# Six of sixteen denominator sums moved from the vector engine to accumulating DMA transfers, with value buffers and early weight work rearranged

## The chip, the cores and the metric

The kernel runs on one core of a Trainium2 chip. The metric is the device time of the whole program in microseconds (us), and lower is better. The time before the change is 3305.59 us, the median of three runs that lie between 3302.00 and 3307.45 us. Five engines work side by side, each in its own program order: PE (matrix products, with PEld for its weight loads), DVE (vector operations), ACT (activations), POOL (GpSimd) and SP (here only an issuer of DMA transfers). They wait for each other by semaphores.

## What is computed

The input is 4 images of 64x64 positions with 256 channels, in fp32. Two layers follow each other:

```python
# layer 0: attention of every position over all 4096 of its image
q = x @ Wq + bq; k = x @ Wk + bk; v = x @ Wv + bv
energy = jnp.einsum('bnd,bmd->bnm', q, k)
attn = softmax(energy, axis=-1)
out = gamma * jnp.einsum('bnm,bmc->bnc', attn, v) + inputs
# layer 1: 3x3 depthwise convolution (three outputs a channel), two pointwise
# layers with a GELU between, a residual, then 3x3 windowed attention and a residual
```

The part that matters here is the softmax of layer 0. The kernel takes exponentials without subtracting a maximum, multiplies them by the values, and divides at the end by the sum of the exponentials, the denominator. `gamma` and the value bias `b_v` enter only where the finished sum is scaled and added to the input.

## The kernel before

The 4 x 4096 positions are cut into 32 **slots** of 512 queries, 8 slots to an image. One slot walks over the 4096 keys of its image in 16 **points** of 256 keys each; a point is named by `G` (0 to 7, a block of 512 keys) and `half`. Number n below is 2G + half. In the loop over points the code writes, in this order: the loads (`load_keys` two blocks ahead, `load_values`, `spread_queries`), `high_part` and `energy` for later points, `load_forms`, the slot's jobs for the second layer (`jobs[point]`, of slots three to five earlier), the product of this point, the sum of the denominators, steps of the depthwise convolution on DVE (`perceive`), and on some slots projections of the next image.

- `energy` (L371) makes two matrix products into a PSUM tile `e`, of which there is one, and ACT's exponential writes `p` (L383), 128 x 1024 numbers. It is called two points ahead of the product, and there are three `p` buffers. So the exponential of n+3 can only be written when everything that reads p of n has ended.
- `product` (L393) adds the values times `p` into PSUM accumulators. At the seven even points 2, 4, ..., 14 of most slots (`IN_PARTS`; not in slots 0, 2 and 31) it does so in three parts, for which DVE makes `pl` (L430) and `pg` (L435) from `p` and ACT's `ph` (L388).
- `add_up` (L421) adds `p` of each point to `den` on DVE (L433). At point 14 it adds p of n = 15 and folds the two halves of `den` (L440). At point 15 `partial_sums` (L450) transposes and reduces `den` to `parts` (L458, L459), together with `lsum`, a sum that POOL makes at point 12 (L1010 to L1020) from masked weights (L991). `finish` (L473) then multiplies `parts` on PE (L477, `dps`), and PE comes to that product straight after point 15.
- `load_values` (L296) fetches a block's values into `v`. There are three such buffers, and the load for block G+2 is written at the start of block G. `load_forms` (L310) fetches the two other forms of the values into `vf`, two buffers, 512 KB a load, three points ahead.
- In slot 0 the values, keys and queries are still being projected (`project_v` L317, `project_qk` L254). `gamma` and `b_v` are loaded on SP's queue just ahead of the first slot (L1107, L1109), and DVE multiplies them at once (L1110, L1112). `clear_tap` (many tiny DVE operations on the convolution's weights) stands at points 5 to 7 of slot 0, and `turn_weights` (four DVE operations of 0.75 us on `wup`, L679) at points 9 to 14. At point 8 of slot 1 POOL stores and reloads weights and makes `wmix` (`mix_weights`, L637).

Each engine executes its instructions in the order in which this code writes them, so a waiting instruction holds up all that is behind it on its engine. A tile with several buffers takes them in turn, and the first write to a buffer waits for its last reader. The lines around the change:

```python
            if half == 0:
                ahead = slot + (G + 2) // NG, (G + 2) % NG
                if ahead[0] < NSLOT:
                    load_keys(*ahead)
                if 0 < ahead[0] < NSLOT:
                    load_values(*ahead)
```

Of the kernel before, what the change touches and what calls it, by code (L numbers as in the profile page):

```python
# [12 lines left out]
ALU = mybir.AluOpType  # L13
# [3 lines left out]
P = 128  # L17
B, H, W, C = 4, 64, 64, 256
# [4 lines left out]
NB = 512  # L23
# [4 lines left out]
TPB = NB // P  # L28
# [5 lines left out]
MULT = 3  # L34
# [5 lines left out]
NG = NT // GRP  # L40
SQ = 32
NJ = NB // SQ
NSLOT = B * NBLK
# [6 lines left out]
SPLIT = 4096.0  # L50
BELOW = 1.0 - 2.0**-13
IN_PARTS = (2, 4, 6, 8, 10, 12, 14)


LAG_PERC, LAG_HID, LAG_ATT = 2, 3, 5
# [3 lines left out]
def attention_then_perception_kernel(  # L59
# [23 lines left out]
    def loaded(src, name, shape=None, queue=None):  # L83
        t = const.tile(list(shape or src.shape), F32, tag=name, name=name)
        (queue or nc.sync).dma_start(out=t, in_=src)
        return t
# [10 lines left out]
    def unshifted():  # L97
# [6 lines left out]
        def tile_of(shape, tag, name, bufs=1):  # L104
            return pool.tile(shape, F32, tag=tag, name=name, bufs=bufs)
# [188 lines left out]
            load_parts(keys[s, G], block(s, G), 1)  # L294

        def load_values(s, G):  # L296
            values[s, G] = tile_of([P, TPB, C], "v", f"v_{s}_{G}", 3)
            to = values[s, G].rearrange("p t c -> p (t c)")
            at = 2 * block(s, G)
            if not any(in_parts(s, G, half) for half in range(2)):  # L300
                nc.sync.dma_start(out=to, in_=packed_v[:, bass.ds(at * 2 * C, TPB * C)])
                return
            for half in range(2):
                if in_parts(s, G, half):
                    of = packed_f[:, at + half, 0]
                else:
                    of = packed_v[:, bass.ts(at + half, 2 * C)]
                nc.sync.dma_start(out=to[:, bass.ts(half, 2 * C)], in_=of)
# [11 lines left out]
        def project_v(s, pair, tag="m"):  # L320
            xc = staged[s]
            ps = bank(tag, f"v_{s}_{pair}")
            for i in range(2):
                for kin in range(CH):
                    nc.tensor.matmul(  # L325
                        ps[:, i * C : (i + 1) * C],
                        lhsT=xc[:, kin, bass.ts(2 * pair + i, P)], rhs=wv[:, kin, :],
                        start=(kin == 0), stop=(kin == CH - 1),
                    )
            of = ps.rearrange("p (t c) -> p t c", c=C)  # L330
            split = 2 * (s % NBLK) + pair in IN_PARTS
            if not split or s < NBLK or s >= NSLOT - NBLK:
                if s >= NBLK:
                    v = fresh(f"vs_{s}_{pair}")
                else:
                    if (0, s) not in values:
                        values[0, s] = tile_of([P, TPB, C], "v", f"v_0_{s}", 3)
                    v = values[0, s][:, 2 * pair : 2 * pair + 2, :]
                nc.scalar.activation(v, of, AF.Identity, scale=SPLIT / (SPLIT + 1.0))  # L339
                nc.scalar.dma_start(  # L340
                    out=packed_v[:, bass.ts(2 * s + pair, 2 * C)],
                    in_=v.rearrange("p t c -> p (t c)"),
                )
            if split:
                low, high = (fresh(f"v{n}_{s}_{pair}") for n in "lh")
                nc.scalar.copy(low, of)
                nc.scalar.activation(high.bitcast(F32R), of, AF.Identity, scale=BELOW)
                nc.vector.tensor_tensor(low, low, high, ALU.subtract)
                gap = fresh(f"vg_{s}_{pair}")
                nc.vector.scalar_tensor_tensor(gap, low, -SPLIT, high, ALU.mult, ALU.add)  # L350
                nc.vector.tensor_scalar(low, low, SPLIT, None, ALU.mult)
                for i, part in enumerate((high, low, gap)):
                    nc.gpsimd.dma_start(
                        out=packed_f[:, 2 * s + pair, i], in_=part.rearrange("p t c -> p (t c)")
                    )
# [9 lines left out]
            load_parts(queries[s], s, 0)  # L365


        weights, highs, lows, gaps = {}, {}, {}, {}
        sums, accs, lsums, lrdens = {}, {}, {}, {}
        parts_, inverses, turneds = {}, {}, {}  # L370

# [2 lines left out]
        def energy(s, G, half):  # L374

            e = epsum.tile([P, 2, NB], F32, tag="e", name=f"e_{s}_{G}_{half}", bufs=1)
            for i in range(2):
                nc.tensor.matmul(  # L378
                    e[:, i, :], lhsT=keys[s, G][:, bass.ts(2 * half + i, P)].bitcast(F32R),
                    rhs=queries[s].bitcast(F32R), start=True, stop=True,  # L380
                )
            p = tile_of([P, 2, NB], "p", f"p_{s}_{G}_{half}", 3)
            nc.scalar.activation(p, e, AF.Exp)  # L383
            weights[s, G, half] = p
# [6 lines left out]
        def product(s, G, half):  # L391
# [17 lines left out]
            for part, (w, to, x) in enumerate((  # L409
                (v, 0, highs[s, G, half]), (f[:, :2], 0, lows[s, G, half]), (f[:, 2:], CH, gaps[s, G, half])  # L410
            )):
                for i in range(2):
                    for c in range(CH):
# [4 lines left out]
                            stop=(to > 0 and n == len(IN_PARTS) - 1 and i == 1),  # L418
                        )

        def add_up(s, G, half):  # L421

            p = weights[s, G, half]
            if G == 0 and half == 0:
                sums[s] = tile_of([P, 2, NB], "den", f"den_{s}")
                return
            if in_parts(s, G, half):
                high = highs[s, G, half]
                low, gap = (tile_of([P, 2, NB], f"p{n}", f"p{n}_{s}_{G}_{half}") for n in "lg")
                nc.vector.tensor_tensor(low.bitcast(F32R), p, high, ALU.subtract)  # L430
            den = sums[s]
            before = weights[s, 0, 0] if (G, half) == (0, 1) else den
            nc.vector.tensor_tensor(den, before, p, ALU.add)  # L433
            if in_parts(s, G, half):
                nc.vector.scalar_tensor_tensor(  # L435
                    gap.bitcast(F32R), low, -SPLIT, high, ALU.mult, ALU.add
                )
                lows[s, G, half], gaps[s, G, half] = low, gap
            if G == NG - 1 and half == 1:
                nc.vector.tensor_tensor(den[:, 0, :], den[:, 0, :], den[:, 1, :], ALU.add)  # L440

        def squares(t):
# [104 lines left out]
            return thirds.pop(0)  # L547

        def spare(s, name):
            if s == NSLOT - 1:  # L550
                return tile_of([P, TPB, C], "v", name, 3).rearrange("p (a t) c -> p a (t c)", a=2)
            spares.append(spares.pop(0))
            return tile_of([P, 2, NB], spares[-1], name)

        spares = ["ph", "pl", "pg"]

        def perceive(s, steps):

# [115 lines left out]
        def turn_weights(n, half):  # L674
            p, q, _ = ROUNDS[n]
            up, uq = (wup1[:, half * MULT + i, :] for i in (p, q))
            swap, back, m = (coef[:, n, i, half : half + 1] for i in range(3))
            for to, k, of in ((uq, back, up), (up, swap, uq), (uq, back, up), (up, m, uq)):
                nc.vector.scalar_tensor_tensor(to, of, k, to, ALU.mult, ALU.add)  # L679
# [424 lines left out]
            project_v(2, i)  # L1104
        fetch(4)
        fetch(5)
        gam = loaded(gamma.partition_broadcast(P), "gam", [P, 1])  # L1107

        gbv = loaded(b_v.rearrange("o (c p) -> p (o c)", p=P), "gbv")  # L1109
        nc.vector.tensor_scalar(gbv, gbv, gam[:, 0:1], None, ALU.mult)  # L1110
        gam_parts = pool.tile([P, 1], F32, tag="gam_parts", name="gam_parts")
        nc.vector.tensor_scalar(gam_parts, gam, 1.0 + 1.0 / SPLIT, None, ALU.mult)  # L1112
        wlv = pool.tile([P, CH, C], F32, tag="wlv", name="wlv")
        combine = combine_steps()

# [8 lines left out]
        for slot in range(NSLOT):  # L1124
# [51 lines left out]
            for point in range(points):  # L1176
                G, half = divmod(point, 2)
                after = slot + (G + 1) // NG, (G + 1) % NG
                if half == 0:
                    ahead = slot + (G + 2) // NG, (G + 2) % NG  # L1180
                    if ahead[0] < NSLOT:
                        load_keys(*ahead)
                    if 0 < ahead[0] < NSLOT:
                        load_values(*ahead)
                    if G == NG // 2 and slot + 1 < NSLOT:
                        spread_queries(slot + 1)
                behind = slot + (point + 1) // points, *divmod((point + 1) % points, 2)
# [1 line left out]
                    high_part(*behind)  # L1189
                if after[0] < NSLOT:  # L1190
                    energy(*after, half)
                soon = slot + (point + 3) // points, *divmod((point + 3) % points, 2)
                if in_parts(*soon):
                    load_forms(*soon)
# [23 lines left out]
                if slot == 0 and point == 1:  # L1218
# [3 lines left out]
                    wperc, bperc = wb[:, :, :, :TAPS], wb[:, :, :, TAPS]  # L1222
                    wup1 = loaded(w_up1, "wup1", queue=nc.gpsimd)
                    bup1 = loaded(b_up1, "bup1", queue=nc.gpsimd)
                if slot == 0 and NG - MULT <= point < NG:
                    if point == NG - MULT:
                        scratch = tile_of([P, NB], "rden", "scratch")
                        scratch = scratch[:, : (TAPS + 3) * CH].rearrange("p (j c) -> p j c", c=CH)
                        nc.vector.tensor_copy(bperc, bias)
                    clear_tap(point - NG + MULT)  # L1230
                if slot == 0 and NG < point <= NG + 2 * MULT:
                    turn_weights(*divmod(point - NG - 1, 2))
                if slot == 0 and point == NG:

                    next(combine)
# [485 lines left out]
```

## Time and profile before

| | |
|---|---|
| median of three runs | 3305.59 us |
| the profiled execution, its whole time | 3305.77 us |
| its span, first to last instruction | 3304.1 us |
| mean granted clock of PE | 0.997 |
| PE busy | 3264.6 us |
| DVE busy | 2905.2 us |
| ACT busy | 1349.2 us |
| POOL busy | 500.7 us |
| denominator sums L433 `den<-den,p`, 448 of them | 564.9 us of DVE |
| DMA, mean rate | 124 GB/s |

1.7 us of the profiled execution lie outside its span. "Busy" counts an engine's own work; issuing a DMA or waiting is not in it for SP and ACT, while POOL's row contains its own DMA issues. In lines of a timeline the first number is the start in us from the span's start, the second the length of the merged run of instructions, then come engine, source line, operation, the tile written `<-` the tiles read, and the count; in brackets stands how long the engine had been idle, and what ended the wait.

### The profile page before, as it was taken

How to read it: one execution, taken by the hardware profiler on the slowest of the kernel's cores; microseconds unless marked ns; L12 is line 12 of the kernel's file. 1: busy time of each engine (PE TensorE's matmuls, PEld its weight loads, DVE VectorE, ACT ScalarE, POOL GpSimd, SP SyncE). 2: the span in 40 equal slices, each digit the busy share in tenths (PEclk: the TensorE clock that was granted, in tenths of full speed). 3: DMA queues.
4: the chain of work that ended last, by engine and by line, in shares of the span. 5: the costliest groups of instructions: out<-in, count | busy, mean ns of one | idle time of the engine just before them, and what ended most of it. 6: DMA issues, size and time to landing. Idle time of an engine off the chain costs nothing.

```text
span 3304.1 us, 35658 instructions
## 1 busy us (share of the span) xinstructions
PE 3264.6 (99%) x11986; PEld 2170.4 (66%) x11986; DVE 2905.2 (88%) x4243; ACT 1349.2 (41%) x1647; POOL 500.7 (15%) x627
## 2 busy tenths in 40 slices
PE   8999999999999999999999999999999999999998
PEld 5556666666666666676666666666666666666655
DVE  4788899888999999987999999998799999999894
ACT  3334444444444444444444444444444444444331
POOL 2200011120111110112001111101210011111121
PEclk9999999999999999999999999999999999999999
DMA  6533333464333433346333333435643333333100
GB/s 207 184 113 108 115 115 117 143 193 139 117 115 122 128 116 114 117 149 209 117 116 117 115 122 121 128 105 174 200 130 103 121 112 115 122 122 121 48 18 27
DMA packets 246910, 410.90 MB, mean 124 GB/s; under 512 B 92272, under 2 KB 93312, under 8 KB 246592
## 3 DMA queue, kind: packets, MB, share of 16 engines
q1 hardware_dynamic: 231632, 370.15, 36.8%
q0 software_dynamic: 7408, 24.95, 1.9%
q10 hardware_dynamic: 7680, 13.44, 1.1%
q8 instruction: 99, 1.62, 0.2%
q14 instruction: 91, 0.75, 0.1%
HBM read 346.92 MB, written 60.69 MB: 123 GB/s over the span
## 4 chain that ended last, share of the span: by engine, by line
PE 92%; DVE 4%; DMA 1%; ACT 1%; issue 1%; SPq 0%; POOL 0%; ACTq 0%; DVEq 0%; POOLq 0%
PE acc L402 30%; PE acc L414 16%; PE e L378 7%; PE dx L762 6%; PE hid_bc L705 5%; PE hid_gf L705 5%; PE hid_de L705 5%; PE lv L925 3%; PE g L858 3%; PE v L325 3%; PE lo L1059 3%; PE s L966 2%; PE hid_a L705 2%; DVE perc L592 2%; PE qk L259 1%; PE hid L737 1%
## 5 line engine op out<-in xcount | busy, mean ns | idle before, releaser
L402 PE MATMUL acc<-p,v 128*128 128x512 f32 x2472 | 1113.5, 593 | 0.2 <-ACT v L339 0.2
L592 DVE SCALAR_TENSOR_TENSOR perc<-xp,wb,perc 128x526 f32<-128x526 f32 (+1 forms) x1356 | 969.1, 773 | 0.1
L383 ACT ACTIVATE p<-e 128x1024 f32<-128x1024 f32 x512 | 524.3, 1024 | 1054.3 <-PE e L378 888.0
L402 PEld LDWEIGHTS acc<-p,v 128*128 128x128 f32 x2472 | 466.8, 190 | 486.8 <-issue 472.5
L433 DVE TENSOR_TENSOR den<-den,p 128x1024 f32<-128x1024 f32 x448 | 564.9, 1261 | 1.0 <-ACT p L383 0.6
L991 POOL TENSOR_TENSOR lp<-lp,near 128x396 f32<-128x396 f32 x60 | 150.8, 2513 | 1965.3 <-ACT lp L986 1965.3
L378 PE MATMUL e<-qa,ka 128*128 128x512 f32 x1024 | 427.9, 499 | 13.0 <-ACT p L383 13.0
L378 PEld LDWEIGHTS e<-qa,ka 128*128 128x128 f32 x1024 | 190.0, 190 | 162.7 <-issue 128.0
L388 ACT ACTIVATE ph<-p 128x1024 fp32r<-128x1024 f32 x203 | 214.4, 1056 | 199.4 <-PE acc L414 130.5
L414 PE MATMUL acc<-ph,v 128*128 128x512 f32 x812 | 264.4, 447 | 0.0
L430 DVE TENSOR_TENSOR pl<-p,ph 128x1024 fp32r<-128x1024 f32 x203 | 253.2, 1247 | 12.1 <-ACT ph L388 12.0
L435 DVE SCALAR_TENSOR_TENSOR pg<-pl,ph 128x1024 fp32r<-128x1024 f32 x203 | 256.7, 1264 | 0.0
L762 PE MATMUL dx<-hid,wup 128*128 128x512 f32 x512 | 229.8, 592 | 0.0
L414 PE MATMUL acc<-pg,vf 128*128 128x512 f32 x812 | 222.0, 395 | 1.1 <-DVE pg L435 1.1
L414 PE MATMUL acc<-pl,vf 128*128 128x512 f32 x812 | 219.6, 392 | 0.0
L414 PEld LDWEIGHTS acc<-ph,v 128*128 128x128 f32 x812 | 148.3, 189 | 51.0 <-issue 26.8
L414 PEld LDWEIGHTS acc<-pg,vf 128*128 128x128 f32 x812 | 152.5, 188 | 37.0 <-DVE pg L435 1.5
L414 PEld LDWEIGHTS acc<-pl,vf 128*128 128x128 f32 x812 | 152.7, 188 | 35.6 <-DVE pl L430 0.4
L598 DVE TENSOR_TENSOR perc<-perc 128x262 f32<-128x262 f32 x360 | 168.0, 481 | 6.3
L1014 POOL TENSOR_TENSOR lsum<-lsum,lp 128x99 f32<-128x99 f32 (+1 forms) x179 | 171.8, 966 | 11.7
L728 ACT ACTIVATE hid<-hid,bup 128x512 f32<-128x512 f32 x120 | 80.1, 715 | 215.8 <-DVE hid L712 215.8
L762 PEld LDWEIGHTS dx<-hid,wup 128*128 128x128 f32 x512 | 96.8, 190 | 98.6 <-issue 93.4
(203 smaller groups left out, 3872.4 us busy)
## 6 DMA issues: line engine op xcount, KB each, us to landing
vf<-packed_f SPq DMA_DIRECT2D x203, 512.0 KB, 4.1
ka<-packed SPq DMA_DIRECT2D x1016, 64.0 KB, 3.0
v<-packed_f SPq DMA_DIRECT2D x203, 256.0 KB, 2.7
v<-packed_v SPq DMA_DIRECT2D x203, 256.0 KB, 2.9
v<-packed_v SPq DMA_DIRECT2D x45, 512.0 KB, 3.5
xp<-in_x SPq DMA_DIRECT2D x30, 528.0 KB, 6.8
xc<-in_x SPq DMA_DIRECT2D x56, 256.0 KB, 3.8
out<-lo SPq DMA_DIRECT2D x56, 256.0 KB, 2.0
```

The costliest lines, as they stand in the source:

```text
L378: nc.tensor.matmul(e[:, i, :], lhsT=keys[s, G][:, bass.ts(2 * half + i, P)].bitcast(F32R), rhs=queries[s].bitcast(F32R), start=True, stop= ...
L383: nc.scalar.activation(p, e, AF.Exp)
L388: nc.scalar.activation(high.bitcast(F32R), weights[s, G, half], AF.Identity, scale=BELOW)
L402: nc.tensor.matmul(accs[s][c], lhsT=v[:, i, bass.ts(c, P)], rhs=p[:, i, :], start=(first and i == 0), stop=(last and i == 1),)
L414: nc.tensor.matmul(accs[s][to + c], lhsT=w[:, i, bass.ts(c, P)].bitcast(F32R), rhs=x[:, i, :].bitcast(F32R), start=(to > 0 and n == 0 and ...
L430: nc.vector.tensor_tensor(low.bitcast(F32R), p, high, ALU.subtract)
L433: nc.vector.tensor_tensor(den, before, p, ALU.add)
L435: nc.vector.scalar_tensor_tensor(gap.bitcast(F32R), low, -SPLIT, high, ALU.mult, ALU.add)
L592: nc.vector.scalar_tensor_tensor(acc, win, wt, acc, ALU.mult, ALU.add)
L705: nc.tensor.matmul(ps[:, n * C : (n + 1) * C], lhsT=w(j), rhs=rows_of(mixes[s, j][:, kind, :]), start=(j == 0), stop=(j == MULT - 1),)
L762: nc.tensor.matmul(ps, lhsT=wup2[:, d, bass.ts(c, P)], rhs=hids[s][:, d, :], start=(d == 0), stop=(d == NHC - 1),)
L1014: nc.gpsimd.tensor_tensor(to, to, near_ws[block, half][:, t_, of, :], ALU.add)
```

## The change

Six of the sixteen sums of a slot, n = 3, 5, 7, 9, 11 and 13 in slots 1 to 30, leave DVE. POOL issues a transfer of `p` into a new tile `sent` instead: a plain copy for n = 3, and transfers that add to what is there for the others. One DVE addition at the end joins `sent` to `den`. The tile `v` has two buffers instead of three, and a block's values are loaded one block ahead instead of two. In slot 0 the eight tiles of values alternate between `v` and `vf`, two buffers each, and of the tiles that slot 31's convolution borrows the third is now a `vf`. `gamma` and `b_v` are loaded after point 1 of slot 0 and multiplied at point 3; `clear_tap` stands at points 3 to 5 instead of 5 to 7, `turn_weights` at points 6 to 11 instead of 9 to 14.

```diff
+BY_DMA = (3, 5, 7, 9, 11, 13)
...
-            values[s, G] = tile_of([P, TPB, C], "v", f"v_{s}_{G}", 3)
+            values[s, G] = tile_of([P, TPB, C], "v", f"v_{s}_{G}", 2)
...
-                        values[0, s] = tile_of([P, TPB, C], "v", f"v_0_{s}", 3)
+                        values[0, s] = tile_of([P, TPB, C], ("v", "vf")[s % 2], f"v_0_{s}", 2)
...
+        def by_dma(s, n):
+            return 0 < s < NSLOT - 1 and n in BY_DMA
+
+        def send(s, n):
+            p = weights[s, n // 2, n % 2]
+            if n == BY_DMA[0]:
+                sent[s] = tile_of([P, 2, NB], "sent", f"sent_{s}")
+                nc.gpsimd.dma_start(out=sent[s], in_=p)
+            else:
+                nc.gpsimd.dma_start(out=sent[s], in_=p, accum_op=ALU.add)
+
         def add_up(s, G, half):
 
+            if by_dma(s, 2 * G + half):
+                return
...
             if G == NG - 1 and half == 1:
+                if s in sent:
+                    nc.vector.tensor_tensor(den, den, sent.pop(s), ALU.add)
                 nc.vector.tensor_tensor(den[:, 0, :], den[:, 0, :], den[:, 1, :], ALU.add)
...
-        gam = loaded(gamma.partition_broadcast(P), "gam", [P, 1])
-
-        gbv = loaded(b_v.rearrange("o (c p) -> p (o c)", p=P), "gbv")
-        nc.vector.tensor_scalar(gbv, gbv, gam[:, 0:1], None, ALU.mult)
         gam_parts = pool.tile([P, 1], F32, tag="gam_parts", name="gam_parts")
-        nc.vector.tensor_scalar(gam_parts, gam, 1.0 + 1.0 / SPLIT, None, ALU.mult)
...
-                    if 0 < ahead[0] < NSLOT:
-                        load_values(*ahead)
+                    if 0 < after[0] < NSLOT:
+                        load_values(*after)
...
                 if after[0] < NSLOT:
                     energy(*after, half)
+                if by_dma(slot, point + 1):
+                    send(slot, point + 1)
...
                     bup1 = loaded(b_up1, "bup1", queue=nc.gpsimd)
-                if slot == 0 and NG - MULT <= point < NG:
-                    if point == NG - MULT:
+                    gam = loaded(gamma.partition_broadcast(P), "gam", [P, 1])
+                    gbv = loaded(b_v.rearrange("o (c p) -> p (o c)", p=P), "gbv")
+                if slot == 0 and MULT <= point < 2 * MULT:
+                    if point == MULT:
+                        nc.vector.tensor_scalar(gbv, gbv, gam[:, 0:1], None, ALU.mult)
+                        nc.vector.tensor_scalar(gam_parts, gam, 1.0 + 1.0 / SPLIT, None, ALU.mult)
...
-                    clear_tap(point - NG + MULT)
-                if slot == 0 and NG < point <= NG + 2 * MULT:
-                    turn_weights(*divmod(point - NG - 1, 2))
+                    clear_tap(point - MULT)
+                if slot == 0 and 2 * MULT <= point < 4 * MULT:
+                    turn_weights(*divmod(point - 2 * MULT, 2))
```

`after` is the block one ahead, (G+1) of the slot, or block 0 of the next slot.

More of the change, by code (lines that the diff above doesn't have):

```diff
@@ L365, in spread_queries @@
             load_parts(queries[s], s, 0)
-        weights, highs, lows, gaps = {}, {}, {}, {}
+        weights, highs, lows, gaps, sent = {}, {}, {}, {}, {}
         sums, accs, lsums, lrdens = {}, {}, {}, {}
@@ L549, in spare @@
         def spare(s, name):
[L550 to L555, printed above, removed]
+            tag = spares[s].pop(0)
+            if tag in ("v", "vf"):
+                return tile_of([P, TPB, C], tag, name, 2).rearrange("p (a t) c -> p a (t c)", a=2)
+            return tile_of([P, 2, NB], tag, name)
+        spares = {NSLOT - 2: ["ph", "pl", "pg"], NSLOT - 1: ["v", "v", "vf"]}
         def perceive(s, steps):
```

## The prediction

> **What bounds the kernel now.** I read the page's busy times and its chain first.
>
> ```profile
> PE 3264.6 (99%) x11986; PEld 2170.4 (66%) x11986; DVE 2905.2 (88%) x4243; ACT 1349.2 (41%) x1647; POOL 500.7 (15%) x627
> ...
> PE 92%; DVE 4%; DMA 1%; ACT 1%; issue 1%; SPq 0%; POOL 0%; ACTq 0%; DVEq 0%; POOLq 0%
> ```
>
> PE is the bound: only 3304.1 - 3264.6 = 39.5 us of its span are idle, and the change leaves PE's instruction list as it is. So the sums taken from DVE can only help where PE waits for DVE. The timeline, cut down to PE's idle brackets, shows where that is. The largest is in slot 0:
>
> ```profile
> 26.76 2.68 SPq L85 DMA_DIRECT2D gam<-in_gamma  x1
> ...
> 29.48 0.50 SPq L85 DMA_DIRECT2D gbv<-in_b_v  x1
> ...
> 30.08 1.89 SPq L223 DMA_DIRECT2D ka<-packed  x4
> ...
> 39.31 0.23 DVE L1110 TENSOR_SCALAR gbv<-gbv,gam 128x2 f32<-128x2 f32 x1 [12.78 <-DMA gbv<-in_b_v]
> ...
> 39.51 1.22 DVE L433 TENSOR_TENSOR den<-p,p 128x1024 f32<-128x1024 f32 x1
> 40.82 1.02 ACT L383 ACTIVATE p<-e 128x1024 f32<-128x1024 f32 x1 [14.28 <-DVE den L433]
> ...
> 41.90 1.22 PE L378 MATMUL e<-qa,ka 128*128 128x512 f32 x2 [8.02 <-ACT p L383]
> ```
>
> DVE stands 12.78 us at the product of the bias, the first sum stands behind it, the exponential waits for that sum to free a `p`, and PE waits 8.02 us for the exponential. The table of windows tells that PE also restarts on a slow clock (the number before the DMA share):
>
> ```profile
> 34.00:42.00 8.00, 0.10 (x1) 0.10 (x1) 2.58 (x4) 1.18 (x2) 0.00 (x0) 0.77 0.47 167
> 42.00:46.00 4.00, 4.00 (x7) 2.11 (x8) 2.92 (x4) 2.02 (x3) 0.00 (x0) 0.60 0.50 151
> ```
>
> The seam of slots 0 and 1 has the next ones (two answers of the timeline):
>
> ```profile
> 115.14 0.69 DVE L440 TENSOR_TENSOR den<-den 128x512 f32<-128x512 f32 x1
> 115.75 3.11 DVE L679 SCALAR_TENSOR_TENSOR wup<-wup,coef 128x512 f32<-128x512 f32 x4
> ...
> 120.34 0.58 PE L477 MATMUL dps<-parts,fold 128*128 128x16 f32 x2 [2.16 <-DVE parts L459]
> ...
> 123.86 3.87 DVE L501 SCALAR_TENSOR_TENSOR xp<-o,gbv,xp 128x512 f32<-128x512 f32 x2
> 125.03 4.37 POOL L637 TENSOR_TENSOR wmix<-wup,wmix 128x768 f32<-128x768 f32 x2
> ...
> 131.65 0.74 PE L378 MATMUL e<-qa,ka 128*128 128x512 f32 x2 [0.56 <-ACT p L383]
> ```
>
> The last turned weights stand between the fold of `den` and its transposes, so PE waits 2.16 us. Then DVE's two L501 take 3.87 us beside POOL's L637 (1.41 us in slot 12), and PE waits 0.56 us here and 1.10 us at 135.55 for `pg`.
>
> After that PE runs without gaps. DVE, though, has no slack at a slot's end; slot 12's:
>
> ```profile
> 1231.01 1.39 DVE L430 TENSOR_TENSOR pl<-p,ph 128x1024 fp32r<-128x1024 f32 x1
> 1232.32 1.39 DVE L433 TENSOR_TENSOR den<-den,p 128x1024 f32<-128x1024 f32 x1
> ...
> 1235.68 1.26 DVE L433 TENSOR_TENSOR den<-den,p 128x1024 f32<-128x1024 f32 x1
> 1236.98 0.69 DVE L440 TENSOR_TENSOR den<-den 128x512 f32<-128x512 f32 x1
> ...
> 1240.08 0.69 DVE L459 TENSOR_REDUCE parts<-turned 128x16 f32<-128x512 f32 x1
> ```
>
> `parts` is done at 1240.77 and PE's `dps` starts at 1241.17: 0.40 us of slack. In six slots it is negative: PE's last product before `dps` then takes about 0.8 us to the next start instead of 0.43 (1047.50 to 1048.30 in slot 10).
>
> **What the Trainium skill says.** "DMA: Bandwidth & Descriptors", "Queues, rings and completion order": a DMA engine serves its queues by turns, a packet at a time, and each ring in order. The trace agrees: SP's tiny `gam`, issued 2.5 us before POOL's 1536 KB `wup`, lands 11.4 us after issue, and the four `ka` behind it took 8.9 us instead of 3.0. Same page, "Anatomy of one DMA": a POOL-issued DMA takes about 2.0 us + bytes/436e3; the 256 KB `packed_f` took 2.9 to 3.6, so the page's 2.6 is low here. It gives no rate for adding transfers. "SBUF — State Buffer", "Who interferes with whom": a DVE operation with two SBUF inputs excludes a POOL operation that reads SBUF; L501 beside L637 agrees. "TensorE: Matmul & The Clock Gate", "What's actually happening": half clock after an idle window of about 3.4 us; above, 0.60 after an 8 us gap.
>
> **The change part by part.**
>
> *Bias and gamma later.* `ka` of block 2 now goes to SP's queue at 26.7 instead of 30.1, ahead of `gam` and `gbv`. DVE's first sum runs at 26.5, so the exponential is ready by 29.6. What is late next is `ka`: before, it landed at 39.0 to 39.9, hidden by the bias. It will still share the engines by turns with `wup` (issued 29.3, landed 38.8). I take 37.0, between 34 (if it escapes `wup`) and 39 (if it drains with it). PE's qk products end at 33.9, so a wait of 3.1 us stays: gain 41.9 - 37.0 = 4.9 (2.9 to 8.0). The slow clock cost 4.54 - 3.43 = 1.1 us on the eight `acc` products and 0.4 on `e`; with a 3 us gap I take it as gone: 1.5 (0 to 1.5). `gbv` should land at about 39; DVE reaches it behind the sum of n = 4, whose exponential ends near 39, so it costs nothing. If it came later, the `p` it holds back isn't rewritten until about 8 us on.
>
> *Weights sooner.* Tap clearing is 3 x 4 us of DVE, now at points 3 to 5, turning 6 x 3.1 us, now at points 6 to 11, where a point lasts about 6 us and DVE has 2 to 4 us of idle time (2.10 before 78.33, 3.83 before 89.53). They cost nothing there; `wup` landed at 38.8. Gone is the 2.16 us wait with about 0.4 of slow clock behind it: 2.6 (2.0 to 2.8). One move isn't named: POOL's storing, reloading and mixing of weights (point 8 of slot 1) now stands behind four sends, so it runs some 25 us later and no longer beside L501. L501 falls by 2.4 us, more than both small waits behind it: start to start 2.4 in all (1.0 to 2.4). Mixing then slows some DVE work of slot 1, where DVE does no convolution.
>
> *Sums.* 180 sums of 1.22 us leave DVE, 30 come back: 183 us of DVE beside PE, worth nothing in themselves. At slot 12's end: the five removed sums after the last wait for PE bring DVE forward by more than 6 us, but `pl` then waits for `ph`, ready at 1229.25. From 1229.4: 1.31 (`pl`), 1.31, 1.53 (`pg`), 0.52, 1.30 (sum n = 15) give 1235.4; the added sum, 1.30 with its dependence, lets the fold start at 1236.7 instead of 1236.98. So it just fits, and the six slots with negative slack gain about 0.4 each: 2.2 (0 to 2.5).
>
> *Sends.* POOL issues 180 DMAs of 512 KB at about 0.54 us (its row for `packed_f`), 97 us on an engine busy for 500.7. The tightest is n = 13: p is ready at about 1221.6, but POOL is in L991 from 1222.54 to 1226.70 with the send behind it. `sent` is needed at 1235.4 + 0.7 of slack, and the freed `p` at about 1236 (the exponential starts at 1234.40, PE's next `e` at 1237.27). So a landing may take 9.3 us from issue. A copy of that size on SP took 4.1 (`vf`); as an addition reads its target too, I estimate twice the data time, 5.4, between 4.1 and 11, since no row bounds it. At 5.4 it is hidden. What the send delays on POOL is L991 and `lsum` by 0.55 us; `lsum` ended 2.2 us before its transpose.
>
> *Two value buffers.* A load is issued at the same place, since it then as now waits for the block before, but is needed two points sooner. Over the 451 loads, issue and landing of before against the earlier product leave 3.9 us at least (slot 23), 12.8 in the middle: nothing, while landings don't grow by 3.9. The borrowed buffers in slots 0 and 31 come free no later.
>
> Sum: 4.9 + 1.5 + 2.6 + 2.4 + 2.2 = 13.6 us of the profiled 3305.77 (1.7 outside its span, unchanged), 3292.2; the median is 0.2 lower, so 3292.0. The ends give 2.9 + 0 + 2.0 + 1.0 + 0 = 5.9 to 8.0 + 1.5 + 2.8 + 2.4 + 2.5 = 17.2: 3288 to 3300, with some 5 more below if the waits for ACT in the projecting slots shrink (2.81 us at 2368.02 is the largest).
>
> **The rivals.** (a) *The start is bound anyway*: `ka` or the bias lands near 40, and one of the small waits stays. For it: `ka` was hardly earlier than the bias. Against: it is now first in its ring. About 3300. (b) *Slower: the adding transfers land late.* Each slot's end, DVE's last sum and the next exponential wait for the send of n = 13. Price: 28 us per us beyond 9.3 (slots 3 to 30), so from 9.8 us on it eats the gain; at 11 us, 28 x 1.7 - 13.6 = +34, 3340. For it: an unmeasured operation behind a 4 us POOL instruction, with DMA at 0.42 share there. Against: POOL's own transfers of half the size need under 4 us. (c) *It doesn't take off what it says*: only if sums were on the path; they are not, so at most (a).
>
> **How the numbers follow.** Main case 0.63 (3292, own range 3283 to 3300), (a) and (c) 0.12, (b) and unseen waits 0.25. Differences within 0.2% (6.6 us) can't be told from no change. The range goes down to 3283 and into (b) to 3328, which leaves out its slower half. Faster 0.63, same 0.12, slower 0.25.
>
> **What would show it.** The wait at L1110 gone and PE's gap near 34 us at about 3; `dps` of slot 0 without a wait; L501 at 1.4 us in slot 1; no wait of DVE or ACT for `sent`; landing of sends under 9 us; DVE busy down by about 180 us. It is wrong if sends land later than that, or if PE shows new waits for `v`.

## The result, and the profile after

The changed kernel takes 3292.32 us (median of five runs, 3291.1 to 3292.78) against 3305.59 us (five runs, 3302.0 to 3309.28): ratio 0.9959, 95% interval 0.9947 to 0.997, so a gain of 0.4% that is clear of the noise. The profiled execution spans 3290.5 us, before 3304.1. In the changed file the same code stands 1 to 17 lines further down (L378 is now L379, L414 L415, L477 L493, L501 L517, L637 L653).

The page, its busy times, chain, groups and DMA issues:

```profile
PE 3263.0 (99%) x11986; PEld 2170.3 (66%) x11986; DVE 2728.5 (83%) x4093; ACT 1349.2 (41%) x1647; POOL 619.9 (19%) x807
...
PE 96%; DVE 1%; issue 1%; ACT 1%; DMA 1%; POOL 0%; SPq 0%; ACTq 0%; DVEq 0%; POOLq 0%
...
L431 POOL DMA_DIRECT2D sent<-p x150 | 129.5, 864 | 1337.5 <-ACT p L384 1328.5
...
L444 DVE TENSOR_TENSOR pl<-p,ph 128x1024 fp32r<-128x1024 f32 x203 | 248.3, 1223 | 66.4 <-ACT ph L389 66.2
...
sent<-p POOLq DMA_DIRECT2D x180, 512.0 KB, 5.2
```

DVE is busy 176.7 us less, PE 1.6 us less, and the span is 13.5 us shorter: as in the profile before, what counts is PE's idle time. The chain, which lay 4% on DVE, has 1% there. `pl` now waits for ACT's `ph`, and the sends land 5.2 us after issue (median).

The start of slot 0, in the timeline:

```profile
26.90 4.14 SPq L224 DMA_DIRECT2D ka<-packed  x4
...
29.36 0.53 POOL L86 DMA_DIRECT2D wup<-in_w_up  x1
...
31.55 0.43 SPq L86 DMA_DIRECT2D gbv<-in_b_v  x1
...
39.08 1.19 PE L379 MATMUL e<-qa,ka 128*128 128x512 f32 x2 [4.27 <-DMA ka<-packed]
...
41.36 1.23 DVE L447 TENSOR_TENSOR den<-den,p 128x1024 f32<-128x1024 f32 x1 [3.39 <-ACT p L384]
42.50 0.22 DVE L1242 TENSOR_SCALAR gbv<-gbv,gam 128x2 f32<-128x2 f32 x1
```

DVE no longer waits for the bias, but PE now waits 4.27 us for `ka`. The merged line stands for four transfers: only the first was issued ahead of POOL's `wup`, the others at 29.64, 30.12 and 30.59 behind it, and the last landed at 38.88, `wup` at 38.69. The same stretch in the table of windows (the number before the DMA share is the granted clock):

```profile
34.00:42.00 8.00, 3.73 (x7) 1.73 (x6) 2.46 (x3) 2.29 (x3) 0.00 (x0) 0.68 1.03 296
42.00:46.00 4.00, 4.00 (x9) 1.87 (x9) 3.49 (x21) 0.04 (x1) 0.00 (x0) 0.79 0.60 134
```

So the slow clock stays, 0.68 and 0.79. These are averages of two values: in the clock records of every trace here the granted clock is either 1 or 0.5, and it changes only after whole multiples of 3.41 us. Windows cut along this grid show what stands ahead of a fall; first three of the kernel before, at the seam and at its wait of 2.81 us late in the program, then two of the changed kernel:

```profile
116.90:120.31 3.41, 1.28 (x3) 0.21 (x3) 3.19 (x5) 0.00 (x0) 0.00 (x0) 1.00 0.54 167
120.31:123.72 3.41, 3.38 (x13) 3.11 (x14) 2.60 (x6) 1.69 (x2) 2.52 (x5) 0.50 0.84 284
...
2366.28:2369.69 3.41, 1.67 (x5) 1.05 (x6) 2.57 (x4) 2.64 (x4) 0.83 (x1) 1.00 0.37 123
```

```profile
33.43:36.84 3.41, 1.38 (x4) 0.19 (x2) 0.70 (x2) 1.26 (x2) 0.00 (x0) 1.00 0.97 337
36.85:43.67 6.82, 4.59 (x7) 2.36 (x8) 3.33 (x11) 1.02 (x1) 0.00 (x0) 0.50 1.07 262
```

The second number is PE's busy time. The clock fell after stretches of the grid in which PE had been idle for about 2 of the 3.41 us. The wait of 2.81 us is cut by the grid into 1.06 and 1.74 us, and the clock stayed at 1. Up to PE's last product, 38 of the 39 falls in the 14 traces follow a stretch with 2.04 us or more of idle time and one (in *wup_later*) a stretch with 1.62 us; no other stretch, the idlest with 2.01 us, was followed by one. The grid lies elsewhere in every execution, so how much a wait of 2 to 5 us costs is partly chance.

The seam of slots 0 and 1:

```profile
114.45 0.69 DVE L475 TENSOR_REDUCE parts<-turned 128x16 f32<-128x512 f32 x1
...
115.77 0.29 PE L493 MATMUL dps<-parts,fold 128*128 128x16 f32 x2
...
119.01 1.41 DVE L517 SCALAR_TENSOR_TENSOR xp<-o,gbv,xp 128x512 f32<-128x512 f32 x2
...
124.27 1.02 PE L379 MATMUL e<-qa,ka 128*128 128x512 f32 x2
```

The three waits are gone: `dps` follows at once, and L517 takes 1.41 us instead of 3.87, since POOL isn't mixing there. Where it mixes now is seen later in slot 1:

```profile
148.32 4.59 POOL L653 TENSOR_TENSOR wmix<-wup,wmix 128x768 f32<-128x768 f32 x2
148.95 2.30 DVE L444 TENSOR_TENSOR pl<-p,ph 128x1024 fp32r<-128x1024 f32 x1 [3.64 <-ACT ph L389]
...
153.92 2.87 DVE L449 SCALAR_TENSOR_TENSOR pg<-pl,ph 128x1024 fp32r<-128x1024 f32 x1
...
156.84 1.19 PE L415 MATMUL acc<-pg,vf 128*128 128x512 f32 x4 [1.04 <-DVE pg L449]
...
167.45 0.89 POOL L431 DMA_DIRECT2D sent<-p  x1 [9.04 <-DMA sent<-p]
...
172.66 1.23 DVE L455 TENSOR_TENSOR den<-den,sent 128x1024 f32<-128x1024 f32 x1 [3.40 <-DMA sent<-p]
```

`pl` and `pg`, 1.23 and 1.22 us elsewhere in this slot, take 2.30 and 2.87, and PE waits for `pg`. The last two lines show a second thing: each send waits for the landing of the one before, and n = 11, issued just behind the loads that follow the mixing, took 9.4 us to land, so n = 13 was issued late and DVE waited for it. ACT, too, waited once there, 2.38 us, for n = 11 to free a `p`. No other wait for a landing send is in the trace. Slot 12's end:

```profile
1216.75 0.88 POOL L431 DMA_DIRECT2D sent<-p  x1
...
1221.02 1.22 DVE L444 TENSOR_TENSOR pl<-p,ph 128x1024 fp32r<-128x1024 f32 x1 [2.04 <-ACT ph L389]
...
1226.94 1.50 DVE L455 TENSOR_TENSOR den<-den,sent 128x1024 f32<-128x1024 f32 x1
...
1231.67 0.69 DVE L475 TENSOR_REDUCE parts<-turned 128x16 f32<-128x512 f32 x1
...
1232.89 0.30 PE L493 MATMUL dps<-parts,fold 128*128 128x32 f32 x2
```

DVE stands idle 2.04 us ahead of `pl`, joins `sent` without a wait, and `parts` is done at 1232.36, 0.53 us ahead of `dps` (before 0.40). PE's last product before `dps` takes 0.43 us to the next start in slots 10, 11, 18, 19, 26 and 27, where it took 0.80 to 0.91. Slot 10 before the change, and PE's line after it:

```profile
1047.56 0.69 DVE L459 TENSOR_REDUCE parts<-turned 128x16 f32<-128x512 f32 x1
1048.30 0.41 PE L477 MATMUL dps<-parts,fold 128*128 128x32 f32 x2 [0.21 <-DMA ka<-packed]
```

```profile
1040.72 0.30 PE L493 MATMUL dps<-parts,fold 128*128 128x32 f32 x2
```

(The bracket names a transfer, but DVE's reduction ended at 1048.25, just ahead of `dps`.)

PE runs the same 11,986 instructions in the same order in both kernels, so the gain up to any of them is the difference of its two starts. By place that gives the table below; its other columns belong to the first four experiments.

| gain in us, by PE's starts | predicted | changed | gamma_alone | weights_alone | sends_alone | no_sends |
|---|---|---|---|---|---|---|
| start, to 46 us of before | 6.4 | 2.3 | 2.3 | -1.5 | -1.8 | 2.1 |
| `dps` of slot 0, products to 124 us | 2.6 | 3.8 | 0.3 | 3.8 | 0.4 | 3.9 |
| `e` and `acc` behind the seam, to 137 us | 2.4 | 2.5 | -0.1 | -1.3 | 1.7 | -1.3 |
| slot 1, to 190 us | 0 | -1.7 | 0.0 | 0.0 | -1.4 | 0.0 |
| 190 to 2300 and 2400 to 3270 us (the six `dps`) | 2.2 | 3.5 | -0.4 | -0.1 | 3.4 | 0.0 |
| 2300 to 2400 us (projecting slots 22 and 23) | 0 | 0.8 | 0.4 | 0.2 | 1.1 | 0.7 |
| PE's tail | 0 | 0.0 | 0.0 | 0.4 | 0.0 | 0.4 |
| after PE's last product | 0 | 2.3 | -0.2 | -0.1 | 2.3 | 0.1 |
| span | 13.6 | 13.5 | 2.3 | 1.3 | 5.6 | 5.8 |

The first row also shows how far two executions differ by chance: sooner weights touch no product up to 42 us of before, and still *weights_alone* lies 1.5 us behind there. Its loads landed later, so that PE went on at 42.85 instead of 41.90, and its clock came back at 47.46 instead of 45.22.

### The profile page after: what moved, and what is told of

Read it like the earlier page. It is cut to its first block, busy times and chain, and to the rows that moved or that the text cites. A ratio compares the mean times of both kernels' runs of the same rounds, so it can differ in the third digit from the quotient of the medians.

```text
span 3290.5 us, 35859 instructions
## 1 busy us (share of the span) xinstructions
PE 3263.0 (99%) x11986; PEld 2170.3 (66%) x11986; DVE 2728.5 (83%) x4093; ACT 1349.2 (41%) x1647; POOL 619.9 (19%) x807
## 3 DMA queue, kind: packets, MB, share of 16 engines
q8 instruction: 99, 1.62, 0.2%
## 4 chain that ended last, share of the span: by engine, by line
PE 96%; DVE 1%; issue 1%; ACT 1%; DMA 1%; POOL 0%; SPq 0%; ACTq 0%; DVEq 0%; POOLq 0%
PE acc L403 32%; PE acc L415 17%; PE e L379 7%; PE dx L778 6%; PE hid_bc L721 5%; PE hid_gf L721 5%; PE hid_de L721 5%; PE lv L941 3%; PE g L874 3%; PE v L326 3%; PE lo L1075 3%; PE s L982 3%; PE hid_a L721 2%; DVE perc L608 1%; PE qk L260 1%; PE hid L753 1%
## 5 line engine op out<-in xcount | busy, mean ns | idle before, releaser
L379 PE MATMUL e<-qa,ka 128*128 128x512 f32 x1024 | 426.8, 498 | 7.6 <-DMA ka<-packed 4.3
L431 POOL DMA_DIRECT2D sent<-p x150 | 129.5, 864 | 1337.5 <-ACT p L384 1328.5
L447 DVE TENSOR_TENSOR den<-den,p 128x1024 f32<-128x1024 f32 x268 | 340.7, 1271 | 9.3 <-ACT p L384 9.1
L379 PEld LDWEIGHTS e<-qa,ka 128*128 128x128 f32 x1024 | 189.8, 189 | 155.9 <-issue 132.3
L415 PE MATMUL acc<-ph,v 128*128 128x512 f32 x812 | 264.7, 447 | 0.0
L415 PE MATMUL acc<-pl,vf 128*128 128x512 f32 x812 | 223.0, 396 | 0.0
L415 PE MATMUL acc<-pg,vf 128*128 128x512 f32 x812 | 219.1, 391 | 1.0 <-DVE pg L449 1.0
L1030 POOL TENSOR_TENSOR lsum<-lsum,lp 128x99 f32<-128x99 f32 (+1 forms) x179 | 197.3, 1109 | 11.7
L1007 POOL TENSOR_TENSOR lp<-lp,near 128x396 f32<-128x396 f32 x60 | 109.2, 1821 | 396.5 <-ACT lp L1002 396.5
L415 PEld LDWEIGHTS acc<-ph,v 128*128 128x128 f32 x812 | 148.2, 189 | 51.2 <-issue 23.0
L415 PEld LDWEIGHTS acc<-pl,vf 128*128 128x128 f32 x812 | 152.8, 188 | 37.1
L415 PEld LDWEIGHTS acc<-pg,vf 128*128 128x128 f32 x812 | 152.5, 188 | 37.4 <-DVE pg L449 1.5
L614 DVE TENSOR_TENSOR perc<-perc 128x262 f32<-128x262 f32 x360 | 155.8, 447 | 8.1
```

Source lines behind the costliest of these rows:

```text
L379: nc.tensor.matmul(e[:, i, :], lhsT=keys[s, G][:, bass.ts(2 * half + i, P)].bitcast(F32R), rhs=queries[s].bitcast(F32R), start=True, stop= ...
L415: nc.tensor.matmul(accs[s][to + c], lhsT=w[:, i, bass.ts(c, P)].bitcast(F32R), rhs=x[:, i, :].bitcast(F32R), start=(to > 0 and n == 0 and ...
L1030: nc.gpsimd.tensor_tensor(to, to, near_ws[block, half][:, t_, of, :], ALU.add)
```

## The experiments

**One part at a time, and the change without its sends.** *gamma_alone* is the kernel before with these edits only:

```diff
-        gam = loaded(gamma.partition_broadcast(P), "gam", [P, 1])
-        gbv = loaded(b_v.rearrange("o (c p) -> p (o c)", p=P), "gbv")
-        nc.vector.tensor_scalar(gbv, gbv, gam[:, 0:1], None, ALU.mult)
...
+                    gam = loaded(gamma.partition_broadcast(P), "gam", [P, 1])
+                    gbv = loaded(b_v.rearrange("o (c p) -> p (o c)", p=P), "gbv")
+                if slot == 0 and point == MULT:
+                    nc.vector.tensor_scalar(gbv, gbv, gam[:, 0:1], None, ALU.mult)
...
```

> Only gamma and the value bias are loaded later and multiplied at point 3. If the start of slot 0 is freed by that alone: PE's wait at the first e after the qk products falls from 8.02 to about 4.3 us and ends at about 39.1 us, bounded by ka, and the time falls by 2.3 to 2.8 us, to about 3303; the rest of the trace is as before (dps of slot 0 waits 2.2 us, L501 beside POOL's mixing). By the prediction's own sizes it would be 4.9 + 1.5 = 6.4 us, 3299.2. If the start is bound anyway, no change.

3302.34 us, ratio 0.9991 (0.9983 to 0.9999). PE goes on at 39.24 us after a wait of 5.39 us for `ka`, and the gain of 2.3 us is all at the start. The first expectation held; the prediction's own size for this part (6.4) did not.

*weights_alone*:

```diff
-                if slot == 0 and NG - MULT <= point < NG:
+                if slot == 0 and MULT <= point < 2 * MULT:
...
-                if slot == 0 and NG < point <= NG + 2 * MULT:
+                if slot == 0 and 2 * MULT <= point < 4 * MULT:
```

> Only the clearing and turning of weights stand 2 and 3 points sooner. If the turned weights were what delayed the fold of slot 0: dps loses its wait of 2.16 us, 2.3 to 2.8 us of gain with the clock behind it, about 3303. POOL's mixing keeps its place in POOL's order, ahead of everything in slot 1, and can start at about 113 us, so L501 and the operations at the seam stay slow and the 2.8 us at e and acc behind them are not gained. Rival: these were gained by the sooner weights too; then 5 to 6 us, about 3300.

3303.26 us, ratio 0.9991 (0.9983 to 1.0), which by itself can't be told from no change. In the trace 3.8 us come at `dps` and the products behind it, more than the 2.8 expected, and 1.3 us go again at the next `e`, since POOL still mixes beside L501.

*sends_alone* has the diff of the change without these two parts.

> Only the six sums by transfers and the two value buffers; gamma, bias and weights as in the kernel before. If the sends' place on POOL moves the mixing: L501 in slot 1's start at about 1.3 us and 2.4 to 2.8 us gained at e and acc behind it, 1.2 us lost in slot 1 where the mixing then runs beside pl, den and pg, and 0.4 to 0.6 us at each of six dps, 3.1 in all: together about 4.5 us, 3301. The 8.02 and 2.16 us waits of slot 0 stay. Rival: the transfers carry most of the change's 13 us; then 3296 or less. Rival: the sends cost more than they bring (later landings); then over 3306.

3299.76 us, ratio 0.9983 (0.9977 to 0.999). It has the fast L517 (1.7 us), slot 1's loss (1.4), the six `dps` (most of 3.4), and the gain after PE's last product. The sum was expected to be 4.5 us; the span is 5.6 us shorter, with 2.3 us at the program's end that the expectation lacks and 1.8 us lost at the start.

*no_sends* is the changed kernel with one line altered:

```diff
-BY_DMA = (3, 5, 7, 9, 11, 13)
+BY_DMA = ()
```

> The changed kernel with all sixteen sums on DVE again; values in two buffers, gamma, bias and weights as changed. Expected: the sum of the other two parts, 5 to 6 us below before, about 3300, with the six dps waits back (3.1 us), the mixing back beside L501 (2.8 us) and slot 1's loss of 1.2 us gone. If two value buffers cost nothing, no PE wait for v appears. Rival: sums off DVE are worth nothing; then it is equal to the changed kernel, 3292.

3298.88 us, ratio 0.9978 (0.997 to 0.9986). All six `dps` are late again (0.82 to 0.91 us), slot 1 loses nothing, PE waits nowhere for `v`, and the seam in its timeline looks like that of before:

```profile
119.13 3.87 DVE L517 SCALAR_TENSOR_TENSOR xp<-o,gbv,xp 128x512 f32<-128x512 f32 x2
...
120.29 4.38 POOL L653 TENSOR_TENSOR wmix<-wup,wmix 128x768 f32<-128x768 f32 x2
...
126.92 0.73 PE L379 MATMUL e<-qa,ka 128*128 128x512 f32 x2 [1.98 <-ACT p L384]
```

The same DVE instruction takes 3.87 us beside POOL's mixing and 1.41 without it. The seam's second gain therefore belongs to the sends, not by what they add up, but because POOL executes in order and the sends hold the mixing back. It also shows why the parts don't add: the sooner weights alone cost 1.3 us there, and the sends take that cost away.

**What holds `ka` back.** *wup_later* is the changed kernel with the big load moved from point 1 to point 4:

```diff
-                    wup1 = loaded(w_up1, "wup1", queue=nc.gpsimd)
-                    bup1 = loaded(b_up1, "bup1", queue=nc.gpsimd)
...
+                if slot == 0 and point == MULT + 1:
+                    wup1 = loaded(w_up1, "wup1", queue=nc.gpsimd)
+                    bup1 = loaded(b_up1, "bup1", queue=nc.gpsimd)
```

> The changed kernel, but the 1536 KB load of wup (and bup behind it) is issued at point 4 of slot 0 instead of point 1, so that it no longer shares the DMA engines with ka of block 2. If wup is what holds ka back: ka lands about 3 us after its issue instead of 7.8, PE's wait of 4.27 us at 39.08 mostly goes (PE goes on at about 35), the clock stays up (about 2 us behind it), and the time falls by 4 to 6 us, to about 3287. Rival: ka is late for another reason (the packed store before it, the xc loads in its own queue); then PE still goes on near 39 and the time stays at 3292.

3287.27 us, ratio to before 0.9941 (0.9927 to 0.9954). The timeline and the windows:

```profile
27.14 2.89 SPq L224 DMA_DIRECT2D ka<-packed  x4
...
35.88 0.73 PE L379 MATMUL e<-qa,ka 128*128 128x512 f32 x2
```

```profile
34.00:42.00 8.00, 8.00 (x25) 3.62 (x25) 4.40 (x14) 3.20 (x4) 0.00 (x0) 1.00 0.51 133
42.00:46.00 4.00, 4.00 (x16) 2.71 (x15) 1.98 (x13) 0.29 (x1) 0.00 (x0) 1.00 0.96 209
```

PE goes on without any wait and at full clock, and the start's gain is 7.6 us instead of 2.3. It was `wup`: `ka` now lands 4.2 to 5.5 us after its issue, not in the 3 us expected, but all of it by 34.26, ahead of PE. This is also what the first row's prediction needed in order to come true.

**Where the mixing should stand.** *mix_sooner* moves POOL's storing and mixing to a place where DVE has nothing to do. The loads of `wup2`, `bup2`, `wlv` and `blv`, which follow in the code, go with `wup2` from point 8 to point 0 of slot 1, also the three that the expectation leaves in place:

```diff
-                if slot == 1 and point == NG:
+                if slot == 0 and point == 4 * MULT:
                     nc.gpsimd.dma_start(out=turned_up, in_=wup1[:, :MULT, C:])
-                    wup2 = loaded(w_up2, "wup2", queue=nc.gpsimd)
                     mix_weights(
                         *blocks_of(wup1, MULT, C), *(wmix[:, i] for i in range(3))
                     )
+                if slot == 1 and point == 0:
+                    wup2 = loaded(w_up2, "wup2", queue=nc.gpsimd)
...
```

> The changed kernel, but POOL's storing and mixing of weights stands at point 12 of slot 0, where DVE has an idle stretch of 7 us, and the loads of wup2, bup2, wlv and blv are as follows: wup2 at point 0 of slot 1, the others where they were. If the mixing beside DVE's pl, den and pg costs slot 1 its 1.2 us, and the loads delay the sends of n = 11 and 13 there (dps 0.26 us late): acc at about 156 us without a wait for pg, 1.2 to 1.5 us less, about 3291. Rival: the mixing slows slot 0's last points or the seam as much; then no gain.

3288.95 us, ratio to before 0.9947 (0.9933 to 0.996). In its timeline the two middle steps of the mixing take 3.71 us instead of 4.59, and slot 1 has no wait for `pg`:

```profile
105.79 3.71 POOL L653 TENSOR_TENSOR wmix<-wup,wmix 128x768 f32<-128x768 f32 x2
...
110.96 0.85 DVE L349 TENSOR_TENSOR vl<-vl,vh 128x512 f32<-128x512 f32 x1 [6.92 <-ACT vh L348]
...
156.66 1.09 PE L415 MATMUL acc<-pg,vf 128*128 128x512 f32 x4
```

Slot 1's loss of 1.7 us is gone (-0.02 by the same reckoning). That `pg` was slow beside the mixing is seen in the lines; how much the moved loads add is not separated. At 60 us of before, ahead of the mixing, this trace lies 1.1 us behind the changed kernel's, since PE went on at 39.38 and the clock came back only at 45.51; from there to the seam the two gain the same, so the rival did not come true. The span is 1.0 us shorter than the changed kernel's, so of the 3.4 us between the medians, more than expected, this trace accounts for 1.0; the two were not timed against each other.

*wup_and_mix* has both edits.

> Both edits of the two kernels ahead of it. If they act in different places, the gains add: 5 to 7 us below the changed kernel, about 3286. Rival: with wup issued later, the turning waits for it and the mixing moves into slot 1 again; then no more than the larger of the two.

3283.60 us, ratio to before 0.9932 (0.9918 to 0.9945), span 3281.4: 9.1 us below the changed kernel's, more than the 5 to 7 expected. By the medians the gains add: 5.1 and 3.4 us for one edit each, 8.7 for both. Its start gains 9.1 us, slot 1 loses nothing. That its start gains 1.5 us more than *wup_later*'s is chance: PE goes on at 34.46 instead of 35.88, because *wup_later*'s trace alone has the slow clock from 21.04 to 24.45.

**What a late send costs.** *send_n15* has n = 15 sent last, and n = 13 added on DVE:

```diff
-BY_DMA = (3, 5, 7, 9, 11, 13)
+BY_DMA = (3, 5, 7, 9, 11, 15)
...
-            nc.vector.tensor_tensor(den, before, p, ALU.add)
+            if not by_dma(s, 2 * G + half):
+                nc.vector.tensor_tensor(den, before, p, ALU.add)
```

> The changed kernel with the last send made of n = 15 instead of n = 13 (DVE adds n = 13). POOL reaches it only behind lsum, at about 1230 us in slot 12, and DVE's L455 needs sent at about 1225.5. If a late landing is priced as the prediction says, each slot with lsum is late by its landing (1230 + 0.9 + about 4.5) less the 1226.9 of now and 0.7 of slack, 7 to 8 us, and slots 1 to 3 by about 2: 27 x 7.5 + 6 = about 210 us more, 3500. Rival: PE and DVE have work that fills the wait (convolution steps, the next e); then much less, under 3 us a slot, below 3380.

3572.16 us, ratio 1.0809 (1.0792 to 1.0825). Timeline of slot 12, and PE's clock behind `dps`:

```profile
1312.00 0.87 POOL L431 DMA_DIRECT2D sent<-p  x1 [0.17 <-issue]
...
1320.98 1.23 DVE L454 TENSOR_TENSOR den<-den,sent 128x1024 f32<-128x1024 f32 x1 [11.21 <-DMA sent<-p]
...
1326.07 0.64 PE L492 MATMUL dps<-parts,fold 128*128 128x32 f32 x2 [8.84 <-DVE parts L474]
```

```profile
1326.00:1330.00 4.00, 3.93 (x10) 3.27 (x11) 3.17 (x8) 1.02 (x1) 0.68 (x2) 0.50 0.02 4
```

Nothing fills the wait. Over all slots PE's start-to-start ahead of `dps` sums to 217 us above 0.43 each, and PE is busy 66.6 us longer (3329.6 against 3263.0), because it goes on at half the clock: 27 slots have a wait of more than 2 us, and in each the clock fell. Together that is 284 us, where the span grew by 278.5. The waits alone came close to the 210 us expected, by errors that cancel: n = 15 landed 8.9 us after issue (median) where 4.5 were taken, so that a full wait is near 9 us instead of 7.5, but it is only some 2.5 us in slots 7, 15 and 23, and slots 1 to 3 lose 1.3 us in all. What the expectation left out is the clock.

**How many sends are needed.** The kernel with both edits, with `BY_DMA` set to `()`, `(13,)` and `(11, 13)`, and last with the two sends in six slots only:

```diff
-            return 0 < s < NSLOT - 1 and n in BY_DMA
+            return s % NBLK in (2, 3) and s > NBLK and n in BY_DMA
```

> Both edits (wup later, mixing sooner) with all sixteen sums on DVE. If the six late dps are all that the sends are worth once the mixing stands elsewhere: 3.1 us back in dps of slots 10, 11, 18, 19, 26 and 27, and 2.2 us at the program's end, whose last DRAIN of POOL took 7.75 us in every trace without sends and 5.54 in every one with them: 5.3 us over the kernel with both edits, 3289. Rival: sums of denominators off DVE bring more (fewer stretched DVE operations all over); then over 3291.

> Both edits, and one send a slot, n = 13, a plain copy. One sum leaves DVE ahead of pl of n = 14 and one, the joining, comes in behind it, so DVE's end of slot is no earlier: the six dps stay late, 0 to 1 us gained against no sends. If any 30 transfers more shorten POOL's last DRAIN it ends at 5.54 us, else (if adding transfers or their number matter) at 7.75. Time 3286 to 3289.

> Both edits, and two sends a slot, n = 11 and 13. If DVE's end of slot is bound by pl of n = 14, which waits for ph about 1.6 us after DVE could now begin it, two sums fewer ahead of it are as good as six: all six dps on time, 3.1 us gained against no sends, the time that of both edits with six sends, 3283.6, at a third of the traffic. Rival: the other four sums matter; then one to three us more.

> Both edits, and the two sends (n = 11 and 13) in slots 10, 11, 18, 19, 26 and 27 alone: 12 transfers in all instead of 60. If the sends are worth just what these six dps wait: PE's last product ends as early as with 60 sends (within 0.5 us), all 32 dps start on time. The time is then 3283.5 but for POOL's last DRAIN, which took 7.75 us with no sends, 2.12 with 30, 5.05 with 60 and 5.54 with 180: 3281 to 3286. Rival: fewer sums on DVE help elsewhere too; then PE ends 1 us or more later than with 60 sends.

The two numbers under "late `dps`" are those of slots 10, 18, 26 and of 11, 19, 27. DRAIN is POOL's long closing instruction, which the views leave out and the traces hold.

| sends | in all | late `dps`, start to start | PE's last product ends | POOL's closing DRAIN | median |
|---|---|---|---|---|---|
| none | 0 | 0.80 and 0.88 us | 3274.76 us | 7.75 us | 3289.62 us |
| n = 13 | 30 | 1.20 and 0.97 | 3276.38 | 2.12 | 3285.30 |
| n = 11, 13 in six slots | 12 | 0.43 | 3272.43 | 4.80 | 3283.23 |
| n = 11, 13 | 60 | 0.43 | 3271.27 | 5.05 | 3283.52 |
| six | 180 | 0.43 | 3270.66 | 5.54 | 3283.60 |

The ratios to before are 0.9956 (0.9939 to 0.9974), 0.9943 (0.9925 to 0.996), 0.9937 (0.9921 to 0.9954), 0.9937 (0.992 to 0.9954), and for six sends the 0.9932 above. One send makes the six `dps` later by 0.1 to 0.4 us, since it takes one sum away and brings the joining in at the slot's end. Two bring all six on time, and the other four sums add at most 0.6 us. By the medians, twelve transfers in the right slots are as fast as 180. PE then ends 1.2 us later than with 60, more than the 0.5 expected, and as late as the expectation's rival asked for. Of this, 0.2 us lie at slot 4's `dps` (0.56 instead of 0.43), which the sends would have served too, and 0.9 between 2364 and 2371 us, in the projecting slots. There PE waits 0.38 us for DVE's `inverse`, which it does neither with 60 sends nor with none, so the number of sums on DVE doesn't explain it; why it waits stays open.

The first row says one more thing. Without a single send, but with `wup` later and the mixing sooner, the kernel takes 3289.62 us, no more than the changed kernel's 3292.32. Against *no_sends* (3298.88), which was timed in another series, the two moved pieces of code bring about 9 us and the 180 sends 6.6.

The last column but one wasn't looked for. After PE's last product, POOL's closing DRAIN took 7.75 us in all five traces without sends, and 5.54 in all six with 180. It isn't a matter of fewer or more: 30 make it 2.12, neither of the two values expected, and so *sends_1* is faster than its range though its six `dps` are later.

## Why the prediction was right

The time was right (3292.0 against 3292.32, inside the range), the mechanism too: PE's waits, not DVE's busy time. But that the sum came out to 0.1 us was luck: its terms were off by up to 2.1 us, and the errors cancel. Term by term:

- *Bias and gamma later, 4.9.* Measured 2.8, and the step that failed is "I take 37.0, between 34 (if it escapes `wup`) and 39 (if it drains with it)". `ka` drained with `wup`, and PE went on at 39.08, the late end. With `wup` out of the way PE went on at 34.4 to 35.9, the other end.
- *Slow clock gone, 1.5.* It cost 0.5 more than before instead. The step that failed is "with a 3 us gap I take it as gone", and not only because the gap became 4.27 us: the clock fell at 36.85, when PE had been idle for 2.0 us, so a PE that went on at 37.0 would have met it too. Before the change PE restarted 3.5 us into the slow stretch and worked through 3.3 us of it; after, it restarted sooner and worked through 4.6. Both terms together: 2.3 for 6.4.
- *Turned weights, 2.6.* Measured 3.8. The 2.2 us of wait were right; the clock behind it, put at 0.4, was 1.5: 3.41 us at half the clock, spread over the transposes that follow.
- *L501 without the mixing, 2.4.* Measured 2.5, and the reason given, that sends stand ahead of POOL's mixing, is shown by the runs with and without sends. The same step said "Mixing then slows some DVE work of slot 1, where DVE does no convolution" and charged nothing: it cost 1.7. Idle time of DVE was no cover, because `pl` and `pg` sit between ACT's `ph` and PE.
- *Sums, 2.2.* Measured 3.5 in those rows, about 3.1 of it at the six `dps`: each was worth 0.5 to 0.6 us, of which 0.37 to 0.48 are the start to start less the 0.43 that remains, and 0.1 follows in the products behind. That DVE is bound by `pl` waiting for `ph`, so that most removed sums buy nothing, held: two sends do what six do.
- *Sends.* Landing 5.2 us median for the estimate of 5.4; for n = 13 6.1. From issue to the joining 10.2 us were there in slot 12, for the predicted 9.3. Issue took 0.86 us for an adding transfer and 0.61 for a plain one, not 0.54. Two of its signs failed in part: in slot 1 DVE waited 3.40 us and ACT 2.38 us for `sent`, and a few sends took up to 9.4 us to land, not under 9. Rival (b) did not come true, with a median of 4.1 us left between landing and joining. But its price was too low: where a send is late by 8 us, the slow clock adds nearly a third to the wait.
- *Two value buffers, 0.* Right: no PE wait for `v` in any trace.
- *Outside the sum.* 2.3 us came after PE's last product, in POOL's DRAIN, a part of the span that the prediction took as unchanged without a word. Its length goes with the number of POOL's transfers; why stays open. The 0.8 us of the projecting slots is no larger than the spread between the traces.

So, to 0.1 us, 4.1 us too much at the start and 1.7 not charged in slot 1 are made up by 1.2 at slot 0's `dps`, 1.3 in the sums' rows, 0.8 in the projecting slots and 2.3 at the end.

## What to carry to other kernels

When a wait is taken away, what is late next may be in the same queue or on the same DMA engines, as `ka` was here: look at what large load was issued within a few microseconds of it, and move that too. When an engine that executes in order gets new waiting instructions, list what stands behind them, and ask beside which work it will now run; here that moved a contention to and fro for 2.5 and 1.7 us. And before taking work off an engine that isn't the bound, find the one instruction at which it is late and count how much has to go ahead of it: two sums in six slots did what 180 transfers did.

## What the runs showed of the hardware

- The Trainium skill, "TensorE: Matmul & The Clock Gate", "What's actually happening", speaks of an idle window of about 3.4 us ahead of the slow clock. The traces agree on the length, with slow stretches of 3.41, 6.83 and 10.24 us, but no stretch has to be idle throughout: about 2.04 us within one were enough. So 2.16 us of idle time ending at 120.34 halved the clock until 123.73, while 2.81 us ending at 2368.02, cut into 1.06 and 1.74, left it at 1.00.
- In the changed kernel a transfer of 512 KB within SBUF issued by POOL lands 3.1 us after issue as a plain copy (n = 3) and 5.0 to 6.1 us as an addition (medians by n); in *send_n15* the last addition, n = 15, takes 8.9 us.
- DVE's `pl`, `pg` and L517 take 1.9 to 2.7 times as long while POOL's subtractions of the mixing run beside them (2.30 for 1.23 us, 2.87 for 1.22, 3.87 for 1.41).
- The closing DRAIN of POOL lasts between 2.12 and 7.75 us, the same to 0.01 us in all traces with the same number of POOL transfers, and in no order by that number (0, 12, 30, 60 and 180 sends: 7.75, 4.80, 2.12, 5.05 and 5.54 us).
